# Centring the first token block of a cross-attention and mixture-of-experts kernel before its scale is known, narrowing its last experts, and moving one expert pair to places 28 and 29

## The chip, the cores and the metric

The kernel runs on one core of a Trainium2 chip. Its time is the device time of one execution in microseconds (us). Before the change the median of six runs is 630.84 us (629.49 to 632.16). The engines are named as the profile names them: PE multiplies matrices (PEld is its weight load), DVE works on vectors, ACT computes activations and copies, POOL computes and issues indirect DMAs, SP issues plain DMAs.

## The reference

2048 tokens of width 512 pass through two layers; everything is float32.

```python
x = x + xattn(layernorm(x), expert = min(clip(itok, 0, 24999) // 6250, 3))
#   xattn: y = (silu(h @ C[e].T) * (h @ C[e].T)) @ C[e].T, C = ctx_2048, one of 4 by token
x = x + ffn(layernorm(x))
#   ffn: residual + top-4 of 32 experts of width 256 (silu(g) * u, then w2, weighted)
#        + one shared expert of width 256, on an rmsnorm of its input
```

The layer norm of the first layer has no learned scale: h = (x - mean) * r, with r = (var + 1e-5) ** -0.5, one r for each token.

## The kernel before

The work has three stages, and PE is meant to run through all of them.

**First layer** (from the start to about 170 us). DVE and PE first sort the tokens by expert (L221 to L265); `ident`, a 128x128 identity, is made on the way (L154), and POOL fills `none`, the source of blank rows, with zeros (L163). `turn_over` (L271) is ten, later five, matmuls on sorted data whose results nobody reads. Then 19 blocks of 128 sorted rows are worked on. For a block b: POOL fetches its rows by an indirect DMA (`x_block`, L332); DVE takes mean and variance (`x_moments`, L344 and L345); DVE adds epsilon and POOL raises to the power -0.5 (`x_root`, L351 and L352); DVE makes the scale and bias `rv` (L407, L410) and ACT applies them (`x_norm`, L426), in block 0 with DVE taking one half (L416); PE transposes the block into PSUM and DVE (in block 0 ACT and DVE, a half each) copies it to `xT` (`turn_block`); `up` (L464) multiplies it with the expert's matrix, of which ACT has copied a part to `held` (`hold`, L395); `gate` takes silu on ACT and the product on DVE; `down` (L485) multiplies back, and DVE adds to the rows (L500). Products of `up` have the matrix as the stationary operand and 128 tokens as the moving one, so their result is already transposed for `down`. Block 0 always uses matrix 0, which is read straight from `cT`. PE's order is up(b+1), transposes of b+2, down(b).

**Routing** (about 90 to 265 us, in part under the first layer): second norm, top 4, row numbers, 64 scatters of rows into a table in DRAM, the shared expert (`glu_up`, `glu_down`, `shared`). `ranks` (L791) sorts the 32 experts by how many rows they have: rank 0 has the most. It also counts experts that have more rows than the kernel's limits; if there are any, a slow general path behind the end runs (L1297).

**Experts** (267 us to the end). The 32 ranks are worked on in the order `ORDER`, each at its place, with the first 256 rows as one tile. `up_rank` (L1072) does 32 matmul instructions of `width(r)` columns: 256, and 240 or 228 for the last ranks (`LOW`). `down_rank_by_halves` (L1114) does 14 of 256 columns, by a scheme with seven products of halves; the last rank is done by `down_rank` (L1148). Ranks 0 to 17 may have more than 256 rows; the rest of two ranks (64 rows each) or four ranks (32 each) goes through one common block (`block_up` L1161, `turn_block_act`, `down_block` L1188) at the place of the first of them. ACT and DVE weight the results into `eo`, and `push` (L1042) adds them to the output by an indirect DMA of POOL: two pushes a rank, three if it has part in a common block. The pushes of one rank wait until those of the rank before have landed. A `drain` of POOL stands ahead of place 29 (L1261).

The order of instructions on an engine comes from a scheduler that follows the program and its dependencies; `behind(a, b)` puts a after b by hand.

Of the kernel before, what the change touches and what calls it, by code (L numbers as in the profile page):

```python
# [17 lines left out]
P = 128  # L18
# [25 lines left out]
LOW = ((26, 240), (29, 228))  # L44
# [4 lines left out]
    + [*range(6, 10), 20, 21, 4, 5, 22, 23]  # L49
    + [*range(10, 14), 24, 25]  # L50
    + [*range(14, 18), *range(26, E)]
# [15 lines left out]
def tile_xattn_moe(  # L67
# [95 lines left out]
    nc.gpsimd.memset(none, 0.0)  # L163
# [177 lines left out]

    def x_moments(j):
        st = small.tile([P, nc.vector.BN_STATS_DIM], F32, tag="st", name=f"st_a{j}")
        ins = nc.vector.bn_stats(st, acc[:, j, :])  # L344
        nc.vector.bn_aggr(xmv[:, j, :], st)  # L345
        return ins

    def x_root(j, n=1):
        js = slice(j, j + n)
        ve = small.tile([P, GT], F32, tag="ve", name="ve")  # L350
        nc.vector.tensor_scalar(ve[:, :n], xmv[:, js, 1], LN_EPS, None, ALU.add)  # L351
        ins = nc.gpsimd.tensor_tensor(xr[:, js], ve[:, :n], mhalf[:, 0, :n], ALU.pow)  # L352
        apart(ins, powers, "of blocks before")
        roots.extend([ins] * n)
        in_turn(ins)
# [4 lines left out]
    downs, ups_, turned, turns, halves = [], [], [], [], []  # L360
# [6 lines left out]
    def x_registers(b):  # L367


        if b == 0:  # L370
            off[0] = 0
            regs[0] = 0, 0
            return None
        with queued(downs[-1] if downs else None):

            off[b] = nc.tensor.value_load(be_i[0:1, b : b + 1], min_val=0, max_val=min(b, EX - 1))
        with queued(adds_x[-1] if adds_x else halves[-1] if halves else None):
            dv = nc.vector.value_load(bl_i[0:1, b : b + 1], min_val=0, max_val=NT - 1)
            loaded = nc.cur_bb.bb.instructions[-1]
        with queued(reads[-1] if reads else None):  # L380
            ac = nc.scalar.value_load(bl_i[0:1, b : b + 1], min_val=0, max_val=NT - 1)
        regs[b] = dv, ac
        return loaded

    def hold(b):

        if b == 0:
            held[0] = cT[:, 0]
            return
        with queued(copies[-1] if copies else None):  # L390
            e = nc.scalar.value_load(be_i[0:1, b : b + 1], min_val=0, max_val=min(b, EX - 1))
        held[b] = ctx_pool.tile([P, DC, D], F32, tag="held", name=f"held{b}", bufs=2)
        n = DC // 2
        for h in range(0, DC, n):
            ins = nc.scalar.copy(  # L395
                held[b][:, h : h + n], cT[:, bass.ds(e, 1), h : h + n].rearrange("p o c f -> p (o c) f")
            )
            apart(ins, matrices[b + 1 :], "of experts that come later")
            copies.append(ins)

    def x_norm(b):
# [12 lines left out]
        n = D // 2 if b == 0 else 0  # L414
        if n:
            scaled = nc.vector.tensor_scalar(  # L416
                hn_[b][:, :n],
                acc[:, bass.ds(dv, 1), :n].rearrange("p o d -> p (o d)"),
                rv[:, 0:1],
                rv[:, 1:2],  # L420
                ALU.mult,
                ALU.add,
            )
            apart(scaled, loads[b + 1 :], "of blocks that come later")
            halves.append(scaled)
# [12 lines left out]
    def turn_block(src, tag, name, eng, after_=None):  # L438
        t = xpool.tile([P, DC, P], F32, tag=tag, name=name)
        if eng is None:  # L440
            n, copies = DC // 2, []
            for h, copy in ((0, nc.scalar.copy), (n, nc.vector.tensor_copy)):
                tp = ps_t.tile([P, n, P], F32, tag="tp", name="tp")
                for c in range(n):
                    ins = nc.tensor.transpose(tp[:, c, :], src[:, (h + c) * P : (h + c + 1) * P], ident)
                copies.append(copy(t[:, h : h + n, :], tp))
            turns.append(ins)
            turned.append(copies[1])
            return t, copies[0]
        tp = ps_t.tile([P, DC, P], F32, tag="tp", name="tp")  # L450
        for c in range(DC):
            ins = nc.tensor.transpose(tp[:, c, :], src[:, c * P : (c + 1) * P], ident)
            if after_ is not None:
                behind(ins, after_)
        turns.append(ins)
        turned.append(nc.scalar.copy(t, tp) if eng is nc.scalar else nc.vector.tensor_copy(t, tp))
        return t

    def up(b, fs, after_=None):
        if fs[0] == 0:  # L460
            ups[b] = ps_m.tile([P, DC, P], F32, tag="mm", name="pp")
        pairs = [(f, c) for f in fs for c in range(DC)] if b else [(f, c) for c in fs for f in range(DC)]
        for f, c in pairs:
            ins = nc.tensor.matmul(  # L464
                ups[b][:, f, :],
                held[b][:, c, f * P : (f + 1) * P],
                xT_[b][:, c, :],
                start=(f == 0 and c == 0) if b == 0 else (c == 0),
                stop=(c == DC - 1),
                skip_group_check=(b == 0),  # L470
            )
            if after_ is not None:
                behind(ins, after_)
        ups_.append(ins)

    def gate(b):
        s = xpool.tile([P, DC, P], F32, tag="s", name="s")
        gated.append(nc.scalar.activation(s, ups[b], AF.Silu))
        aT_[b] = xpool.tile([P, DC, P], F32, tag="aT", name="aT")
        made[b] = nc.vector.tensor_tensor(aT_[b], s, ups[b], ALU.mult)  # L480
# [24 lines left out]
    def xattn():  # L505
# [4 lines left out]
        fetched(0, 1, 2)  # L510
        for b in range(2):
            loaded = x_registers(b)
            with tc.issue_after(loaded) if loaded is not None else nullcontext():
                st = x_moments(b)
            behind(st, scaled if b else planned)
            if not b:
                turn_over(5, st)
            x_root(b)
            fetched(3 + b)
            scaled = x_norm(b)  # L520
            if b:
                behind(reads[-1], half_)
            else:
                xT_[0], half_ = turn_block(hn_[0], "xT", "xT", None)
        hold(0)
        up(0, range(DC - 1))
        hold(1)
        xT_[1] = turn_block(hn_[1], "xT", "xT", nc.vector, ups_[0])
        up(0, range(DC - 1, DC), turns[-1])
        gate(0)  # L530
        hold(2)
        for b in range(2, GT):
            st = x_moments(b)
            behind(st, turned[b - 2])
            behind(st, scaled)
            x_root(b)
            fetched(3 + b)
        fetched(GT + 3)
        x_norm(2)
        behind(powers[-1], turned[1])  # L540
        for b in range(XB):
            j = GT * (b // 2 + 1)
            if not b:
                behind(x_moments(GT), made[0])
                x_moments(GT + 1)
            elif j < NT and b % 2 == 0:
# [3 lines left out]
            if b + 3 < XB:  # L550
                x_norm(b + 3)
                if not b:
                    behind(powers[-1], made[0])
            if 0 < b < XB - 2:
                hold(b + 2)
            if b + 1 < XB:
                up(b + 1, range(DC // 2))

# [3 lines left out]
            if b + 1 < XB:  # L562
                up(b + 1, range(DC // 2, DC))
                gate(b + 1)
                if not b:
                    behind(reads[-1], gated[-1])
            n = b - (XB - NT) - 2
            if n >= 0:
                row_ = turn_row(n, ups_[-1])
            if b + 2 < XB:  # L570
                xT_[b + 2] = turn_block(hn_[b + 2], "xT", "xT", nc.vector)
            if not b:
                for i in range(GT + 2, 2 * GT):
                    st = x_moments(i)
                    behind(st, turned[-1])
                x_root(GT, GT)
# [214 lines left out]
    def ranks():  # L791
# [35 lines left out]
        lim = slots.tile([P, E], F32, name="lim")  # L827
        more = slots.tile([P, E], F32, name="more")
        nc.vector.tensor_scalar(lim, rank, float(XA), float(XWA - XWB), ALU.is_lt, ALU.mult)
        nc.vector.tensor_scalar(more, rank, float(XZ), float(XWB), ALU.is_lt, ALU.mult)  # L830
        nc.vector.scalar_tensor_tensor(lim, lim, float(CM), more, ALU.add, ALU.add)
        had = CM
        for r, n in LOW:
            nc.vector.tensor_scalar(more, rank, float(r), float(had - n), ALU.is_ge, ALU.mult)
            nc.vector.tensor_tensor(lim, lim, more, ALU.subtract)
            had = n
        nc.vector.tensor_tensor(lim, n_e, lim, ALU.is_gt)
        over = slots.tile([P, 1], F32, name="over")
        nc.vector.tensor_reduce(over, lim, AX.X, ALU.add)
        over_i = const.tile([P, 1], I32, name="over_i")  # L840
        nc.vector.tensor_copy(over_i, over)
        return er, er_x, er_i, over_i
# [69 lines left out]
    er, er_x, er_i, over_i = ranks()  # L912
    for g in range(G):
        if g:
            aT_s[g], _ = glu_up(h2T[g], shw13, f"s{g}")
        shared(g, aT_s[g])
    while to_put:
# [225 lines left out]
    def down_rank(aT, w2t, wt, to, n, r):  # L1143
        for j in range(MJ):
# [6 lines left out]
            eo = weighted(po, wt[:, j : j + 1], f"{r}_{j}", "eo", m)  # L1151
# [272 lines left out]
```

## Time and profile before

| what | value |
|---|---|
| median of six runs | 630.84 us |
| the profiled execution | 631.29 us |
| its span, first to last instruction | 629.4 us, so 1.9 us lie around it |
| PE, DVE, POOL, ACT busy | 605.5, 401.7, 246.8, 216.5 us |
| first matmul of the sort | 3.91 us |
| first product of block 0 (`up`) | 17.32 us |
| first product of block 1, from which PE is busy | 22.55 us |
| experts' first matmul | 267.40 us |
| last matmul ends | 620.80 us |
| last push issued | 622.01 us |

The page gives each engine's busy time and slices of the span. A timeline lists instructions in order: start, duration, engine, line, operation, what is written from what, and in brackets how long the engine had been idle and what released it. The view of waits adds up such idle times. The chain of waits follows the end back to the start.

### The profile page before, as it was taken

The page shows a single profiled execution, that of the slowest core. Times are in us where ns is not written, and L with a number is a line of the kernel's source. Part 1 is how long each engine was busy: PE and PEld are TensorE (multiplying, and loading weights), DVE is VectorE, ACT ScalarE, POOL GpSimd, SP SyncE. Part 2 cuts the span into 40 slices and gives each one's busy share as a digit, 9 for nine tenths or more (in the row PEclk, how much of TensorE's full clock was granted, in tenths as well). Part 3 has the DMA queues.
Part 4 walks back from the last instruction along what each step waited for, and adds up shares of the span by engine and source line. Part 5 has one row for each costly group of instructions (what it writes and reads, how often), then busy time and mean ns, then how long its engine had stood idle before and what let it go on. Part 6 is the DMA issues. An engine that isn't in the chain of part 4 may idle for free.

```text
span 629.4 us, 10438 instructions
## 1 busy us (share of the span) xinstructions
PE 605.5 (96%) x2962; PEld 434.5 (69%) x2962; DVE 401.7 (64%) x1113; ACT 216.5 (34%) x390; POOL 246.8 (39%) x217
## 2 busy tenths in 40 slices
PE   5899999999996999999999999999999999999994
PEld 2777767777542444477688688858868886888882
DVE  7655556676633822576577677776776778678770
ACT  2435666655321000023222323323332332333331
POOL 4461002366673465414333324234233342524323
PEclk9999999999996999999999999999999999999998
DMA  7489993326272497799989999999999999999434
GB/s 254 148 306 406 414 415 125 120 103 223 103 272 108 171 368 241 210 287 289 299 207 214 272 287 211 215 287 224 248 285 243 212 218 289 237 273 228 68 50 56
DMA packets 104450, 144.55 MB, mean 230 GB/s; under 512 B 21184, under 2 KB 58048, under 8 KB 101824
## 3 DMA queue, kind: packets, MB, share of 16 engines
q1 hardware_dynamic: 86400, 101.54, 53.9%
q0 software_dynamic: 17984, 42.26, 27.5%
q8 instruction: 26, 0.43, 0.3%
q14 instruction: 40, 0.33, 0.2%
HBM read 79.05 MB, written 66.22 MB: 231 GB/s over the span
## 4 chain that ended last, share of the span: by engine, by line
PE 73%; issue 7%; POOL 6%; DVE 5%; DMA 4%; SPq 2%; another core or an unknown queue 1%; ACT 0%; POOLq 0%; DVEq 0%
PE pg L1072 17%; PE pu L1072 16%; PE po L1114 15%; PE pp L464 6%; PE po L485 6%; POOL s_dram L652 4%; PE pp_x L1161 3%; PE po L870 3%; PE pg L855 2%; SPq L940 2%; PE po L1188 2%; PE pu L855 2%; DMA out<-eo,to_all 2%; DMA acc<-in_x,xtok 1%
## 5 line engine op out<-in xcount | busy, mean ns | idle before, releaser
L1042 POOL DMA_INDIRECT out<-eo,to_all x64 | 101.6, 1588 | 218.1 <-DVE eo L1120 95.3
L1072 PE MATMUL pg<-xT,w 128*128 128x256 f32 (+2 forms) x512 | 135.5, 377 | 0.0
L1117 ACT ACTIVATE eo<-po,wt 128x256 f32<-128x256 f32 x124 | 58.4, 473 | 167.1 <-PE po L1114 141.7
L1072 PE MATMUL pu<-xT,w 128*128 128x256 f32 (+2 forms) x512 | 114.0, 376 | 0.0
L1072 PEld LDWEIGHTS pg<-xT,w 128*128 128x128 f32 x512 | 96.6, 190 | 18.5 <-issue 6.2
L1072 PEld LDWEIGHTS pu<-xT,w 128*128 128x128 f32 x512 | 97.3, 190 | 11.5
L652 POOL DMA_INDIRECT s_dram<-h,slot x64 | 62.1, 970 | 36.0 <-issue 16.5
L464 PEld LDWEIGHTS pp<-xT,held 128*128 128x128 f32 x576 | 66.8, 192 | 8.0 <-issue 5.2
L464 PE MATMUL pp<-xT,held 128*128 128x128 f32 x576 | 68.2, 276 | 1.1 <-DVE st_b L611 0.6
L485 PE MATMUL po<-cT,aT 128*128 (+1 forms) x152 | 68.4, 592 | 0.0
L993 DVE STREAM_TRANSPOSE xT<-z 128x1024 f32<-128x1024 f32 x32 | 65.1, 2034 | 0.0
L1120 DVE SCALAR_TENSOR_TENSOR eo<-po,wt,eo 128x256 f32<-128x256 f32 x93 | 45.0, 484 | 24.5 <-PE po L1114 19.8
L1079 DVE TENSOR_TENSOR aT_r<-s,pu 128x256 f32<-128x256 f32 (+2 forms) x64 | 26.5, 414 | 39.0 <-PE pu L1072 30.1
L485 PEld LDWEIGHTS po<-cT,aT 128*128 128x128 f32 x152 | 27.4, 190 | 27.3 <-issue 27.3
L1003 ACT ACTIVATE xT<-xT,nwq 128x256 f32<-128x256 f32 x64 | 29.0, 500 | 46.2 <-DVE xT L993 29.2
L618 POOL TENSOR_TENSOR rs<-rs,mhalf 128x2 f32<-128x2 f32 x16 | 11.3, 704 | 73.0 <-DVE rs L617 73.0
L1095 DVE TENSOR_TENSOR t_r<-w,t_r 128x256 f32<-128x256 f32 x62 | 26.3, 425 | 21.1 <-PE po L1114 20.8
L395 ACT COPY held<-cT 128x1024 f32 x36 | 36.0, 1047 | 10.3 <-DVE valid L312 10.0
L1114 PE MATMUL po<-w,aT_r 128*128 128x256 f32 x124 | 37.8, 386 | 0.1
L1114 PE MATMUL po<-t_r,s_r 128*128 128x256 f32 x124 | 37.6, 385 | 0.0
L1114 PE MATMUL po<-t_r,aT_r 128*128 128x256 f32 x124 | 37.3, 382 | 0.0
L870 PE MATMUL po<-shw,aT_s 128*128 128x512 f32 x64 | 32.8, 651 | 1.5 <-issue 1.1
(203 smaller groups left out, 766.2 us busy)
## 6 DMA issues: line engine op xcount, KB each, us to landing
w<-in_w SPq DMA_DIRECT2D x192, 256.0 KB
s_dram<-none SPq DMA_DIRECT2D x1, 20840.0 KB
z<-s_dram SPq DMA_DIRECT2D x128, 128.0 KB
h_dram<-h SPq DMA_DIRECT2D x4, 1042.0 KB
cT<-in_ctxT SPq DMA_DIRECT2D x4, 1024.0 KB
out<-none SPq DMA_DIRECT2D x1, 1024.0 KB
s_dram<-h,slot POOLq DMA_INDIRECT x64
out<-eo,to_all POOLq DMA_INDIRECT x64
```

What stands on the lines that cost most here:

```text
L395: ins = nc.scalar.copy(held[b][:, h : h + n], cT[:, bass.ds(e, 1), h : h + n].rearrange("p o c f -> p (o c) f"))
L464: ins = nc.tensor.matmul(ups[b][:, f, :], held[b][:, c, f * P : (f + 1) * P], xT_[b][:, c, :], start=(f == 0 and c == 0) if b == 0 else (c ...
L485: ins = nc.tensor.matmul(po, aT_[b][:, f, :], cT[:, bass.ds(off[b], 1), f, :].rearrange("p o f -> p (o f)"), start=(f == 0), stop=(f == DC ...
L652: put = nc.gpsimd.indirect_dma_start(out=table, out_offset=bass.IndirectOffsetOnAxis(ap=index, axis=0), in_=src, in_offset=None,)
L870: ins = nc.tensor.matmul(po, aT[:, f, i * P : (i + 1) * P], w2t[:, f, :], start=(f == 0), stop=(f == IC - 1))
L993: ins = nc.vector.transpose(xT.rearrange("p c (r b) -> p r c b", b=SQ), z.rearrange("p r (a c) -> p r c a", c=DC))
L1003: on_act.append(nc.scalar.mul(xT[:, c, :], xT[:, c, :], nwq[:, c : c + 1]))
L1042: put = nc.gpsimd.indirect_dma_start(out=out, out_offset=bass.IndirectOffsetOnAxis(ap=dst, axis=0), in_=eo, in_offset=None, bounds_check=T ...
L1072: last_up = nc.tensor.matmul(ps, w13t[:, c, f * P : (f + 1) * P], xT[:, c, :n], start=(c == 0), stop=(c == DC - 1))
L1114: return nc.tensor.matmul(ps, L[i], R[i], start=first_, stop=True, skip_group_check=True)
L1117: nc.scalar.mul(eo[i][:, j, :], ps, wt[:, i : i + 1])
L1120: return nc.vector.scalar_tensor_tensor(eo[i][:, j, :], ps, wt[:, i : i + 1], eo[i][:, j, :], ALU.mult, ALU.add)
```

## The change

1. **First block.** Its rows are only centred, half on DVE and half on ACT (`x_centre`); the scale follows later, at the gate (`x_scale`, `gate`). Its `up` is now four products with tokens as the stationary operand and all 512 columns of the matrix moving; the gated result is transposed afterwards by PE (`turn_first`). Both copies of its transposes are ACT's. Block 1 is normed by halves on DVE and ACT and copied by halves on ACT and DVE. Four blocks are fetched ahead, not three; later moments, roots and copies move, and `turn_over` after the first moments is two matmuls, not five.
2. **Blank rows**: `none` is zeroed by ACT, not by POOL.
3. **Narrower last ranks**: `LOW` has widths from rank 20 on. The limits' count, which grows by ten instructions, moves from `ranks` to behind the second group of the shared expert (`limits`).
4. **Order**: ranks 4 and 5, with their common block, go from places 12 and 13 to places 28 and 29; later ones move up.
5. **Last rank**: its results are weighted by halves on ACT and DVE.

```diff
-LOW = ((26, 240), (29, 228))
+LOW = ((20, 252), (22, 248), (24, 244), (26, 240), (28, 234), (29, 228), (30, 224))
 ORDER = (
     [0, 1, 2, 3, 18, 19]
-    + [*range(6, 10), 20, 21, 4, 5, 22, 23]
-    + [*range(10, 14), 24, 25]
-    + [*range(14, 18), *range(26, E)]
+    + [*range(6, 10), *range(20, 24)]
+    + [*range(10, 14), *range(24, 27)]
+    + [*range(14, 18), *range(27, 30)]
+    + [4, 5, 30, 31]
 )
...
-    nc.gpsimd.memset(none, 0.0)
+    nc.scalar.mul(none.rearrange("p j w -> p (j w)"), ones16[:, 0:1].to_broadcast([P, NB * RW]), 0.0)
...
+    def x_centre():
...
+        nc.vector.tensor_scalar(neg[:, 0:1], xmv[:, 0, 0:1], -1.0, None, ALU.mult)
+        hn_[0] = xpool.tile([P, D], F32, tag="hn", name="hn")
+        n = D // 2
+        scaled = nc.vector.tensor_scalar(hn_[0][:, :n], acc[:, 0, :n], xmv[:, 0, 0:1], None, ALU.subtract)
+        halves.append(scaled)
+        reads.append(nc.scalar.activation(hn_[0][:, n:], acc[:, 0, n:], AF.Identity, bias=neg[:, 0:1]))
...
+    def x_scale():
+        ins = nc.vector.tensor_tensor(first_[0][:, 1:2], xr[:, 0:1], valid[:, 0:1], ALU.mult)
...
+                    ps, left, right = ups[b].rearrange("p f t -> p (f t)"), xT_[b][:, c, :], cT[:, 0, c, :]
...
+        gated.append(nc.scalar.activation(s, ups[b], AF.Silu, scale=by))
+        made[b] = nc.vector.scalar_tensor_tensor(s, ups[b], by, s, ALU.mult, ALU.mult)
...
+    def turn_first(after_):
+        aT_[0] = turn_block(first_[1].rearrange("p f t -> p (f t)"), "aT", "aT", nc.vector, nc.vector, after_=after_, whole=True)
...
-        fetched(0, 1, 2)
...
+        fetched(0, 1, 2, 3)
+        st = x_moments(0)
+        behind(st, planned)
+        turn_over(2, st)
+        scaled = x_centre()
+        xT_[0] = turn_block(hn_[0], "xT", "xT", nc.scalar, nc.scalar)
+        half_ = turned[-1]
+        x_root(0)
+        loaded = x_registers(1)
+        with tc.issue_after(loaded):
+            st = x_moments(1)
+        behind(st, scaled)
+        x_root(1)
+        fetched(4)
+        scaled = x_norm(1)
+        behind(reads[-1], half_)
+        behind(x_scale(), scaled)
+        halves.append(scaled)
+        up(0, range(DC - 1))
+        hold(1)
+        xT_[1] = turn_block(hn_[1], "xT", "xT", nc.scalar, nc.vector, after_=ups_[0])
...
+        up(0, range(DC - 1, DC), turns[-1])
+        hold(2)
+        behind(copies[2], first_half)
...
                 up(b + 1, range(DC // 2, DC))
+                if not b:
+                    turn_first(ups_[-1])
                 gate(b + 1)
...
+        if g == 1:
+            over_i = limits(adds_s[-1])
...
-            eo = weighted(po, wt[:, j : j + 1], f"{r}_{j}", "eo", m)
+            eo = last.tile([P, D], F32, tag="eo", name=f"eo_{r}_{j}", bufs=EO)
+            nc.scalar.mul(eo[:m, :HD], po[:m, :HD], wt[:m, j : j + 1])
+            nc.vector.tensor_scalar(eo[:m, HD:], po[:m, HD:], wt[:m, j : j + 1], None, ALU.mult)
             push(eo[:m, :], to[:m, j : j + 1], f"rank{r}")
```

## The prediction

> **What bounds the kernel now.** I read the page first, then PE's waits, then timelines of the three places that the change touches.
>
> ```profile
> PE 605.5 (96%) x2962; PEld 434.5 (69%) x2962; DVE 401.7 (64%) x1113; ACT 216.5 (34%) x390; POOL 246.8 (39%) x217
> ...
> PEclk9999999999996999999999999999999999999998
> ```
>
> PE is busy for 605.5 of 629.4 us. PE's waits cut to the experts' stage (266 to 622 us) have a single entry of 0.3 us: there every column that PE doesn't process is time saved, and work of other engines costs nothing while PE has no wait. The other 24 us lie at three places: before PE has steady work (22.55 us), at 187 to 203 us (the dip to 6 in the clock row), and after its last matmul (8.6 us). The change works on the first and the third, and on PE's column count.
>
> **The head: POOL's fill.** A stretch of the timeline from 1.4 us:
>
> ```profile
> 1.26 0.28 DVE L148 TENSOR_SCALAR tri<-iota_q,row_b 128x128 f16<-128x128 f32 x1
> ...
> 1.53 1.99 DVE L154 TENSOR_SCALAR ident<-iota_q,row_b 128x128 f32<-128x128 f32 x1
> 1.59 1.85 POOL L163 MEMSET none<- 128x2084 f32 x1
> ...
> 2.44 1.19 DVE L226 TENSOR_SCALAR ge<-tok_sb 128x16 f16<-128x16 int32 x3
> ```
>
> `ident` takes 1.99 us where its twin `tri` takes 0.28, and it ends just after POOL's memset. The first `ge` starts at 2.44 and is held until 3.54 (1.10 us, the two others 0.10 and 0.15). With the fill on ACT, the three `ge` end near 2.8 instead of 3.63, and all that follows (matmul at 3.91, sort, first fetch on POOL at 10.07) comes some 0.85 us sooner. Bounds: nothing, if something else holds DVE, and 1.0, if the `ge` were instant. ACT's fill is about 2.1 us (a copy of 1024 columns takes 1.05) and lies in ACT's idle time from 2.2 to 12.2 us; without that cover it would delay `held`. Does the fetch land sooner too? In windows of 1 us the three matrices keep the DMA at 393 GB/s until 11 us and leave 80 GB/s in the next; the rows' packets would start about there. I pass on the whole 0.85; nothing is the other end. The Trainium skill ("DMA: Bandwidth & Descriptors", Queues, rings and completion order) says that a DMA engine takes turns between rings packet by packet, which speaks against this step: sharing the last 0.3 us of the matrices' traffic would take some 0.15 us from it, an estimate.
>
> **The first block.** From the timeline of 13.5 to 23 us:
>
> ```profile
> 13.71 0.69 DVE L344 BATCH_NORM_STATS2 st_a<-acc 128x6 f32<-128x512 f32 x1 [1.41 <-DMA acc<-in_x,xtok]
> 14.44 0.18 DVE L345 BATCH_NORM_AGGREGATE xmv<-st_a 128x2 f32<-128x6 f32 x1
> ...
> 14.90 0.58 POOL L352 TENSOR_TENSOR xr<-ve,mhalf 128x1 f32<-128x1 f32 x1 [1.12 <-DVE ve L351]
> ...
> 15.90 0.41 DVE L416 TENSOR_SCALAR hn<-acc,rv 128x256 f32<-128x256 f32 x1
> ...
> 16.96 0.69 DVE L344 BATCH_NORM_STATS2 st_a<-acc 128x6 f32<-128x512 f32 x1 [0.65 <-DMA acc<-in_x,xtok]
> ...
> 17.32 2.90 PE L464 MATMUL pp<-xT,cT 128*128 128x128 f32 x24
> ...
> 17.57 0.41 DVE L446 COPY xT<-tp 128x256 f32<-128x256 f32 x1
> ...
> 19.62 0.81 ACT L426 ACTIVATE hn<-acc,rv 128x512 f32 x1 [1.07 <-DVE rv L410]
> 20.49 0.66 PE L452 MATMUL tp<-ident,hn 128*128 128x128 f32 x4 [0.28 <-ACT hn L426]
> ...
> 22.55 0.71 PE L464 MATMUL pp<-xT,held 128*128 128x128 f32 x4 [0.50 <-DVE xT L456]
> ```
>
> Block 0: from the end of the moments (14.62) to DVE's half (16.31) pass 1.69 us, through `ve`, POOL's power and two `rv`. Centred, it is a negation (next start some 0.1 later) and the same 0.41: 0.55. So `up(0)` starts 1.1 earlier by this and 0.85 by the head: about 15.35. But its first three products last only 6 x 0.43 = 2.6 us (a 512-column instruction starts every 0.43 in L485's rows); PE is then through at 17.95 and block 1 is late next.
>
> Block 1 therefore sets the gain. Today its moments start at 16.96, on landing, and its `up` at 22.55: 5.59 us. In it DVE copies a half of block 0 (17.57), which pushes `ve` back; block 0's undisturbed rows take 2.19 from moments to `hn` (13.71 to 15.90), block 1's 2.66. ACT does the whole block (0.81), and DVE's copy waits behind another block's moments (0.50 of PE). After: 2.19, ACT's half 0.60, two transposes with their starts 0.3, the last product of `up(0)` 0.86, under which both copies (0.37 and 0.41) hide: 3.95. That is 1.64 less, so with the head `up(1)` starts at 22.55 - 0.85 - 1.64 = 20.06, after a PE gap of about 0.8 us. If the scheduler sets a `held` copy of 1.05 ahead of `hn`, the gap covers most of it; without the gap it costs 1.05.
>
> Against it stand the four transposes of `turn_first`: 4 x 0.11 = 0.44 on PE. Its DVE copies (0.41 each) lie under the four transposes of block 2. The four wide products replace 32 short instructions (3.57 us) by 8 x 0.43 = 3.44, inside what is counted. Sum of the front: -0.85 - 1.64 + 0.44 = **-2.05**; its ends are -0.8 (fetch unmoved, a little lost to order) and -2.6. POOL's root of block 3 now waits for `turn_first`'s copies, so fetches 6 and 7 are issued some 1.7 later (26.07 to 27.8) and block 4 is normed by about 35 us; PE transposes it near 39. Without those 4 us it would cost what is missing. The blank rows' 20.8 MB go out about 1.2 later, and the first scatter at 120.80 has room.
>
> Fewer `turn_over` matmuls are off the path. They matter for the clock: ten took 4.45 us at 9.83, the next five 1.33 from 14.46, half the time each. The Trainium skill ("TensorE: Matmul & The Clock Gate", Part 1 and Part 4) has the full clock follow one busy window of about 3.4 us that runs free, and transposes not count as busy. This speaks against fewer matmuls and a gap: one window late would cost up to 1.7 us, an estimate; the ten matmuls alone are longer than a window. No term here uses it.
>
> **Narrower ranks.** From PE's timeline:
>
> ```profile
> 556.94 3.62 PE L1072 MATMUL pu<-xT,w 128*128 128x256 f32 x16
> ...
> 576.30 3.40 PE L1072 MATMUL pu<-xT,w 128*128 128x240 f32 x16
> ...
> 604.75 3.24 PE L1072 MATMUL pu<-xT,w 128*128 128x228 f32 x16
> ```
>
> From `pu` to the next `pu` a plain rank takes 9.93 us at 256 columns (388.89 to 398.82), 9.57 at 240 (566.73 to 576.30), 9.37 at 228 (604.75 to 614.12): 22 and 20 ns a column. The change takes 4, 8 and 12 columns from two ranks each, 6 from rank 28 and 4 from 30 and 31. 54 x 22 ns = 1.2; for the last eight I take 0.05, as 228 columns cost 192 ns an instruction and the weight load beside it 190. Sum **-1.25**, from -1.1 to -1.67 (62 x 32 x 0.84 ns). Six more memsets of 95 ns lie in DVE's 36% of idle time. By the reference's routing the ranks 20 to 31 have 247, 245, 243, 240, 240, 239, 229, 223, 221, 210, 201 and 195 rows, within the new widths, so the general path doesn't run. `limits`, 21 short DVE instructions of some 0.2, goes into DVE's idle 6.25 us ahead of 232.27; SP reads the result at 231.3 and its next rows are fetched at 242, so it costs nothing; without that room it would hold the z fetches.
>
> **The pair and the end.** A common block costs PE the same anywhere. Its cost is in pushes:
>
> ```profile
> 605.04 1.55 POOL L1042 DMA_INDIRECT out<-eo,to_all  x1 [6.88 <-issue]
> ...
> 612.63 1.55 POOL L1042 DMA_INDIRECT out<-eo,to_all  x1 [4.17 <-DVE eo L1120]
> ...
> 619.11 0.69 ACT L1037 ACTIVATE eo<-po,wt 128x512 f32<-128x512 f32 x1 [4.19 <-PE po L1148]
> ...
> 620.14 1.56 POOL L1042 DMA_INDIRECT out<-eo,to_all  x1 [4.09 <-ACT eo L1037]
> ```
>
> The last ranks' first pushes are 7.59 and 7.51 us apart: 1.86 between the two, then landing (619.36 in the chain of waits) and 0.78 to the next. PE's results come 8.98 apart, then 7.81. With three pushes the spacing is 10.4 to 11.0 where loads run (545.65, 556.67, 567.08, 577.87). At place 29 the loads are over (SP's last is at 580.61), and a third of 64 rows adds about 1 us: 8.5, below 9. I take 8.5, the quiet rows being nearer; at 10.8 rank 31 is 1.5 late. The drain ran to 604.17, some 7.6 after the last push before it; after place 28 the common block's 6.7 us of PE cover that. The last weighting falls from 0.69 to 0.48, but the push at 620.14 waits also for the landing at 619.36: **-0.1**, between -0.3 and +1.5.
>
> **Sum.** -2.05 - 1.25 - 0.1 = -3.4. The profiled execution, 631.29 us with 1.9 around the span, lies 0.45 above the median of 630.84; it would become 627.9 (span 626.0), the median **627.4**. About 0.2% (1.26 us) is what a measurement can tell from no change.
>
> **How it could go.**
>
> - *As summed*, 0.52: 627.4, own range 626.2 to 629.1 by the ends above.
> - *The front gives nothing*, 0.16: the fetch lands no sooner (+0.85) and the first block runs at the half rate of the ten matmuls (+1.5 of its 3.4 us): 629.8. For it: the same DMA engines carry the fourth matrix; against: DMA falls to 80 GB/s at 11 us.
> - *Pushes hold the end*, 0.11: 10.8 between ranks 5 and 30, +1.5: 628.9.
> - *The stall at 187 us goes*, 0.06: PE does next to nothing from 189 to 196 with no wait that explains it. Its loss is some 9 us; a different instruction stream may miss it: 618.
> - *Slower*, 0.15: the clock falls between the second `turn_over` and `up(1)`. In windows around the stall it is 0.86 at 190 to 193, 0.50 to 200, 0.60 to 203, so about 10.2 us at half, from 192.2 on, after a stretch from 188.8 almost without matmuls. In the front that costs up to 5.1: 632.5, and more than 3.4 from about 6.8 us at half clock. It decides once the gap of 0.8 us grows to some 3 (block 1's rows landing 2 us late). Against it: no such gap today.
>
> Faster: 0.52 + 0.06 + 0.09 of the push case + 0.04 of the second = 0.71; same: 0.12 + 0.02 = 0.14; slower 0.15. The range leaves out the stall's case (0.06) and most of the slower one (0.12): 625.8 to 631.4.
>
> **What will show it.** Right: `ident` near 0.3 us, first fetch near 9.2, `up(0)` near 15.4, `up(1)` near 20.1, 9.57 or less from place to place for ranks 20 to 31 where they have no block, last push some 3.4 earlier. Wrong: `ident` still 2 us; moments of block 1 still at 16.96; a clock below 1 before 30 us; more than 9 us between the first pushes of ranks 5 and 30; new PE waits after 30 us.

## The result and the profile after

The changed kernel takes 632.0 us (median of 20 runs, 630.86 to 634.01), the kernel before 630.29 us (46 runs, 628.77 to 632.16). The ratio is 1.003, with a 95% interval of 1.0022 to 1.0037: slower by 0.3%. The forecast was 627.4 us, its range 625.8 to 631.4. The profiled execution took 632.07 us, with a span of 630.3; that of the kernel before, at 631.29, lies 1.0 above its median, so the two profiles differ by 0.8 us where the medians differ by 1.7.

One thing is needed to read the numbers below: the kernel before took 630 to 632 us beside the runs above and beside seven of the experiments, and 622 us beside the other eight, one chip showed both, and every ratio is to the kernel before in the same set of runs ("beside 630" and "beside 622" say which).

The page, to be held against the two rows of before:

```profile
PE 605.4 (96%) x2939; PEld 433.6 (69%) x2939; DVE 405.3 (64%) x1133; ACT 219.8 (35%) x394; POOL 245.5 (39%) x216
...
PEclk9998999999996999999999999999999999999998
```

The 23 instructions less are the shorter `turn_over` (3) and the wide products (24), with the four transposes of `turn_first` added, and the sum of PE's busy time hardly moved. The clock row has a new 8 in its fourth slice, at 47 to 63 us. The front itself, from the timeline (start, duration, and in brackets how long the engine had been idle and what released it):

```profile
1.54 0.28 DVE L155 TENSOR_SCALAR ident<-iota_q,row_b 128x128 f32<-128x128 f32 x1
2.48 0.33 DVE L227 TENSOR_SCALAR ge<-tok_sb 128x16 f16<-128x16 int32 x3 [0.66 <-DMA tok_sb<-in_tok]
...
13.15 0.69 DVE L347 BATCH_NORM_STATS2 st_a<-acc 128x6 f32<-128x512 f32 x1 [1.68 <-DMA acc<-in_x,xtok]
...
15.52 2.79 PE L484 MATMUL pp<-cT,xT 128*128 128x512 f32 x6
...
19.80 3.73 PE L484 MATMUL pp<-xT,held 128*128 128x128 f32 x32
...
24.27 0.44 PE L464 MATMUL tp<-ident,s 128*128 128x128 f32 x2 [0.52 <-DVE aT L468]
```

Up to block 1's `up` at 19.80 (22.55 before) all of it came within 0.3 us of the forecast. Then PE's milestones turn round:

| start of | before | after | difference |
|---|---|---|---|
| `up` of block 0 | 17.32 | 15.52 | -1.80 |
| `up` of block 1 | 22.55 | 19.80 | -2.75 |
| `down` of block 0 | 26.66 | 24.98 | -1.68 |
| `up` of block 3 | 37.53 | 35.85 | -1.68 |
| `up` of block 4 | 45.09 | 47.12 | +2.03 |
| `up` of block 5 | 52.61 | 56.26 | +3.65 |
| experts' first matmul | 267.40 | 270.78 | +3.38 |
| first `pu` of the last rank | 614.12 | 616.12 | +2.00 |
| last push | 622.01 | 624.20 | +2.19 |
| end of the span | 629.4 | 630.3 | +0.9 |

So the change gains 1.68 us in the front, loses 5.33 between 39 and 56 us, gets 0.27 back up to the experts and 1.38 from the first rank to the last, loses 0.19 up to the last push and gains 1.29 behind it. The loss in the timeline, engine by engine:

```profile
39.43 0.60 PE L464 MATMUL tp<-ident,hn 128*128 128x128 f32 x4
39.86 3.60 PE L507 MATMUL po<-cT,aT 128*128 x8
43.61 0.96 POOL L333 DMA_INDIRECT acc<-in_x,xtok  x1 [0.30 <-issue]
45.52 0.60 ACT L492 ACTIVATE s<-pp 128x512 f32<-128x512 f32 x1 [5.58 <-remote]
46.28 0.69 DVE L468 COPY xT<-tp 128x512 f32<-128x512 f32 x1 [7.33 <-remote]
47.12 1.64 PE L484 MATMUL pp<-xT,held 128*128 128x128 f32 x11 [3.66 <-ACT held L391]
```

PE's transposes of block 4 stand at 39.43 to 40.03, and the copy of their result starts at 46.28. DVE had been idle for 7.33 us; what released it is given as "remote", that is, the trace found no instruction. The trace's records of PE's signals stand at 45.50 and 46.26, just ahead of the two starts, so the two engines were released by PE, late. ACT's silu of block 3 had waited 5.58 us for products that PE's records end at 39.59. PE then waits 3.66 us for the copy (the label names ACT's `held`; the copy at 46.28 to 46.97 is what ends last). The line of POOL is the last of eight fetches in a row, 34.72 to 44.57. After the wait the clock falls. By windows (the window and its length, the busy time of PE, PEld, DVE, ACT and POOL with their instructions, the granted clock, the DMA share, GB/s):

```profile
48.20:51.70 3.50, 3.50 (x19) 3.50 (x18) 3.29 (x11) 0.00 (x0) 0.07 (x1) 0.51 0.67 269
```

That is 3.5 us at half clock: block 4's 32 products and the transposes to the next start take 5.44 us, not 3.81. That is 3.66 + 1.63 = 5.29 of the 5.33.

The kernel before had the same late results in the same place, and hardly a wait. Its timelines of POOL, ACT, DVE and PE:

```profile
41.32 0.96 POOL L332 DMA_INDIRECT acc<-in_x,xtok  x1 [0.30 <-issue]
...
44.25 0.60 ACT L478 ACTIVATE s<-pp 128x512 f32<-128x512 f32 x1 [7.27 <-remote]
...
42.90 0.69 DVE L344 BATCH_NORM_STATS2 st_a<-acc 128x6 f32<-128x512 f32 x1 [0.34 <-DMA acc<-in_x,xtok]
...
44.25 0.69 DVE L456 COPY xT<-tp 128x512 f32<-128x512 f32 x1
...
45.09 1.13 PE L464 MATMUL pp<-xT,held 128*128 128x128 f32 x8
```

Its row of fetches ends at 42.28, its transposes at 41.71, and PE's signals for silu and copy are recorded at 44.17 and 44.23. But here the copy could hardly have come sooner: DVE has the moments of the fetched rows ahead of it, waits for their landing (42.90) and is busy until 44.13. Beside 622 us (`before_again`) silu starts at 40.73 with no such delay, and the copy still only at 43.79. The changed kernel has these moments behind the copy, so there PE's late signal is all that the copy waits for. PE's `up` at 45.09 follows the start of the `down` ahead of it by 3.55 us, where its neighbours take 3.43 or 3.44: it was already 0.12 us late.

### The profile page after: what moved, and what is told of

It is laid out like the page before. It is cut to its first block, busy times and chain, and to the rows that moved or that the text cites. A ratio compares the mean times of both kernels' runs of the same rounds, so it can differ in the third digit from the quotient of the medians.

```text
span 630.3 us, 10421 instructions
## 1 busy us (share of the span) xinstructions
PE 605.4 (96%) x2939; PEld 433.6 (69%) x2939; DVE 405.3 (64%) x1133; ACT 219.8 (35%) x394; POOL 245.5 (39%) x216
## 4 chain that ended last, share of the span: by engine, by line
PE 68%; issue 10%; POOL 7%; DMA 6%; DVE 4%; another core or an unknown queue 2%; ACT 1%; POOLq 0%; ACTq 0%; DVEq 0%
PE pg L1118 15%; PE pu L1118 14%; PE po L1160 13%; PE pp L484 6%; PE po L507 4%; DMA out<-eo,to_all 4%; PE po L914 4%; POOL s_dram L690 3%; PE pu L899 3%; PE pg L899 3%; PE pp_x L1209 3%; PE po L1236 1%; DMA acc<-in_x,xtok 1%; POOL out L1088 1%
## 5 line engine op out<-in xcount | busy, mean ns | idle before, releaser
L1118 PE MATMUL pg<-xT,w 128*128 128x256 f32 (+7 forms) x512 | 134.9, 375 | 0.0
L1118 PE MATMUL pu<-xT,w 128*128 128x256 f32 (+7 forms) x512 | 113.1, 374 | 0.0
L484 PEld LDWEIGHTS pp<-xT,held 128*128 128x128 f32 x576 | 68.5, 196 | 11.4 <-issue 5.1
L484 PE MATMUL pp<-xT,held 128*128 128x128 f32 x576 | 69.7, 280 | 4.2 <-ACT held L391 3.7
L1125 DVE TENSOR_TENSOR aT_r<-s,pu 128x256 f32<-128x256 f32 (+7 forms) x64 | 26.4, 412 | 37.0 <-PE pu L1118 32.6
L1141 DVE TENSOR_TENSOR t_r<-w,t_r 128x256 f32<-128x256 f32 x62 | 26.5, 427 | 21.2 <-PE po L1160 20.8
```

The costliest lines, as they stand in the source:

```text
L484: ins = nc.tensor.matmul(ps, left, right, start=(c == 0), stop=(c == DC - 1))
L1118: last_up = nc.tensor.matmul(ps, w13t[:, c, f * P : (f + 1) * P], xT[:, c, :n], start=(c == 0), stop=(c == DC - 1))
```

## The experiments

Theory A: the row of eight indirect DMAs holds back PE's results (or PE) until about its end. The change ends the row 2.3 us later, in part since POOL's root of block 3 waits for the copies of `turn_first` (without the two lines that order this, `root3_early_2` below ends it 1.1 sooner), and wants the result 1.7 us sooner. Theory B: the mere traffic of the DMA engines does it, which were full from 36 to 47 us. Theory C: the order of the work around block 4.

**The first four runs** came beside a kernel before of 622.03 us. `split`:

```diff
-                fetched(*range(2 * GT, NT))
+                fetched(*range(2 * GT, 3 * GT))
                 second_inputs(st)
-                blanks(loads[-1])
+            if b == 3:
+                for j in range(3 * GT, NT):
+                    x_block(j)
+                    behind(loads[-1], adds_x[-1], mybir.DependencyClass.Sync)
+                blanks(loads[-1])
```

> The changed kernel with the last eight fetches of rows cut in two: blocks 8 to 11 as before, blocks 12 to 15 (and the blank rows that wait for them) only after block 2's rows are added. In the changed kernel PE stands from 43.46 to 47.12, then runs at half clock for 3.4 us; the results that DVE and ACT wait for came 5.9 us after the matmuls that the trace shows. Theory A (the eight indirect DMAs of POOL in a row, 34.72 to 44.56, hold back PE's results or PE itself until about their end): with four of them the release comes near 40, PE has no wait before block 4's up, its up stands near 43.5 instead of 47.12, no half clock near 48, time 632.0 - 5.3 = 626.7. Theory B (the amount of DMA traffic, the shared expert's weights above all): the wait stays to within 1.5 us, 630.5 or more. Theory C (the order of DVE's and ACT's work around block 4): nothing changes, 632.

`inputs_late`:

```diff
-                second_inputs(st)
                 blanks(loads[-1])
+                second_inputs(loads[-1])
```

> The changed kernel with the loads of the shared expert and the blank output rows (2.6 MB, on SP at 31.9 to 35.6 us) issued behind the long write of blank rows instead of ahead of it; the eight fetches in a row stay. Theory A (the eight fetches in a row): PE's wait before block 4's up stays, 3 to 3.7 us, 632. Theory B (DMA traffic: 16 engines full at 36 to 47 us in the changed kernel, and not without these loads): the wait goes, up of block 4 near 43.5, no half clock near 48, 626.7. Theory C (order of work): nothing changes, 632.

`root3_early`:

```diff
-                    behind(aggrs[3], turned[-1])
...
-                    behind(made[1], ves[3])
```

> The changed kernel without the two lines that put block 3's variance and its epsilon behind the copies of the turned first block, so that POOL's root of block 3, the fetches 6 and 7 and the eight fetches after them come about 1.2 us sooner. Theories A and B alike: the release of PE's results moves with the burst, from 45.5 and 46.3 to about 44.3 and 45.1, PE waits 1.2 us less (2.4 us) and may keep its clock: 629 to 631. If the lateness of the burst is not what costs (theory C), 632.

`back_only` is the kernel before with the parts 3 to 5 of the change alone:

```diff
-LOW = ((26, 240), (29, 228))
+LOW = ((20, 252), (22, 248), (24, 244), (26, 240), (28, 234), (29, 228), (30, 224))
...
-    + [*range(14, 18), *range(26, E)]
+    + [*range(14, 18), *range(27, 30)]
+    + [4, 5, 30, 31]
```

> The kernel before with only the narrower ranks, the new order, the moved count of limits and the last rank's halves; first layer as before. My prediction's terms give 630.3 - 1.25 - 0.1 = 628.9. The changed kernel's trace, compared place by place, gives 1.38 from the first to the last rank and 1.1 at the end that may be chance: 628.9 or 627.8. If these parts cost, and not the first layer, it is 631 or more.

Measured: split 617.51 us, ratio 0.9921 (0.9906 to 0.9935); root3_early 617.83, 0.9931 (0.9915 to 0.9948); back_only 619.97, 0.9959 (0.9943 to 0.9975); inputs_late 648.67, 1.0416 (1.0398 to 1.0434). None of the four shows a wait before block 4's `up`, and none the dip of PE at 187 us that before has. So split and root3_early tell nothing apart here. inputs_late missed for a reason of its own, which its waits of PE name:

```profile
PE tp L464 <- ACT h2T L686: 26.7, 1, 26.7
```

The norm weights lay behind 20.8 MB on SP's queue, and ACT needed them for `h2T`. back_only gives 2.1 us: more than the 1.35 of my terms.

**The kernels themselves in such a set.** `after_again` and `before_again` are without edits; `front_only` is the kernel before with the parts 1 and 2 of the change:

```diff
-    nc.gpsimd.memset(none, 0.0)
+    nc.scalar.mul(none.rearrange("p j w -> p (j w)"), ones16[:, 0:1].to_broadcast([P, NB * RW]), 0.0)
...
-        fetched(0, 1, 2)
+        fetched(0, 1, 2, 3)
```

`inputs_mid` has the second inputs in another place:

```diff
-                second_inputs(st)
-                blanks(loads[-1])
+            if b == 3:
+                last_ = second_inputs(adds_x[-1])
+                behind(blanks(loads[-1]), last_)
```

> The changed kernel itself, once more, with a profile. In the last four runs the kernel before took 622.0, not 630.3, and no variant showed PE's dip at 187 us or a wait at 43 us. Theory D (what cost at 43 to 52 us is a standstill of PE's results that some chips or executions show and others don't, not the change's own work): where the kernel before takes about 622, the changed kernel has no wait before block 4's up and takes 622.0 - 2.0 (back) - 1.7 (front) = 618.3; where before takes about 630, PE's wait of 3.7 and the half clock are there again, 632. Theory A (the burst is late by itself): wait there on any chip, 623.5 where before takes 622.

> The kernel before itself, for a profile on the same chip as its neighbours. Theory D: if it takes about 622, no dip of PE at 187 to 203 us and full clock there; if it takes about 630, the dip as in the first profile.

> The kernel before with only the changes of the first layer (centred block 0, blank rows filled by ACT); order, widths and last rank as before. By the trace of the changed kernel the front gains 1.68 us up to block 3, and then loses 5.3 at 39 to 52 us. Where the kernel before takes about 622: 620.3 by theory D, 625.6 by theory A. Where it takes about 630: 634 by both.

> The changed kernel with the loads of the shared expert, the norm weights and the blank output rows (2.6 MB) only after block 2's rows are added, and ahead of the long write of blank rows; the eight fetches in a row stay. (In inputs_late they came behind that write, and PE waited 26.7 us for the norm weights; here they come ahead of it.) Where the kernel before takes about 630: by theory A (eight fetches in a row) PE's wait of 3.7 us before block 4's up stays, 632; by theory B (DMA traffic) it goes, 626.7. Where it takes about 622 there is no such wait in any case by theory D: 618.3, as the changed kernel.

Measured, beside a kernel before of 622.08: **after_again 617.92 us, ratio 0.9938 (0.9922 to 0.9954)**, before_again 622.11, front_only 621.81, 0.9993 (0.9981 to 1.0004), inputs_mid 617.8, 0.9929 (0.9914 to 0.9944). The same changed kernel that is slower by 0.3% beside 630 is faster by 0.6% beside 622. In its profile the copy that started at 46.28 starts right behind the transposes (39.21 to 39.81), though POOL issues the same row, here until 44.23, and the DMA engines are as full (0.98 to 1.08 from 36 to 46 us):

```profile
39.84 0.69 DVE L468 COPY xT<-tp 128x512 f32<-128x512 f32 x1 [1.05 <-PE tp L464]
43.08 3.18 PE L484 MATMUL pp<-xT,held 128*128 128x128 f32 x27
```

PE has no gap. Theory C falls, since the order is the same, and theories A and B fall as causes that act in every run. Theory D holds: the standstill is there in some runs and not in others. What is left to tell apart is what brings it where it is there. Held instruction by instruction against after_again, PE in the recorded execution falls back at two places only, by 5.5 us at 43 to 52 and by 9.2 at 186 to 205. front_only missed: 621.8, not 620.3. Its profiled execution has PE's last matmul 1.40 us before that of before_again and a span 2.6 shorter, but the other runs spread from 620.3 to 623.2, and why is open.

**Beside 630 us.** split again:

> The kernel of split once more, for where the kernel before takes about 630 us (in the runs so far beside it took 622, and neither it nor the changed kernel showed a wait at 43 us or a dip at 187). Where before takes about 630: theory A (the eight indirect DMAs in a row bring the standstill of PE's results) says no wait before block 4's up, 626.7, ratio 0.994; theory B (traffic of the DMA engines as such) says a wait of more than 2 us and a ratio of 1.000 to 1.003. Where before takes 622: 617.5 as the first time, and nothing is told apart.

Measured: 627.48 us beside 631.07, **ratio 0.9932 (0.9909 to 0.9956)**. POOL, DVE and PE:

```profile
39.45 0.96 POOL L333 DMA_INDIRECT acc<-in_x,xtok  x1 [0.30 <-issue]
...
41.60 0.69 DVE L468 COPY xT<-tp 128x512 f32<-128x512 f32 x1 [1.50 <-PE tp L464]
...
44.11 3.73 PE L484 MATMUL pp<-xT,held 128*128 128x128 f32 x32
```

The row ends at 40.41, the copy starts 1.19 later, PE does not wait, and the clock stays whole there. The DMA engines were full until 46 us (1.03 in the window of 42 to 44). So B falls, and the row is left, as theory A says. The dip at 187 to 201 us is there.

Then the other half, the row without the traffic:

> The kernel of inputs_mid again (the changed kernel with the 2.6 MB of second inputs only after block 2's rows are added; the eight fetches in a row stay), for where the kernel before takes about 630 us. There, split had no wait at 43 us although the DMA engines were full until 46 us, so traffic alone does not bring the standstill. If the row of eight indirect DMAs alone brings it: the wait of 2 to 3.7 us before block 4's up stays, ratio 1.000 to 1.003. If it takes both, the row and full DMA engines: no wait, ratio about 0.993. Where before takes 622: 617.8, and nothing is told apart.

Measured: 632.43 us beside 631.4, ratio 1.0025 (1.0009 to 1.0041). By windows the DMA engines are 0.56 to 0.70 busy from 36 to 46 us, and PE's wait before block 4's `up` is 3.75 us:

```profile
42.00:44.00 2.00, 1.43 (x4) 0.36 (x2) 0.00 (x0) 0.00 (x0) 1.39 (x3) 1.00 0.67 213
```

The row brings it without full DMA engines. Next, whether the wait lasts as long as the row. `row6` is split with 6 and 2 fetches for 4 and 4:

```diff
-                fetched(*range(2 * GT, 3 * GT))
+                fetched(*range(2 * GT, 3 * GT + 2))
...
-                for j in range(3 * GT, NT):
+                for j in range(3 * GT + 2, NT):
```

> The changed kernel with the row of eight fetches cut to six, the last two (and the blank rows) after block 2's rows are added. If PE's results are held until the row ends (44.56 in the changed kernel, first result at 45.50): the row ends near 42.0, results come at 42.5 to 43.9, PE waits at most 1.5 us before block 4's up (3.66 in the changed kernel) and its clock stays whole: ratio about 0.993 to 0.996 where the kernel before takes 630. If a hold of fixed length starts after some number of DMAs under seven: wait still over 3 us, 1.000 to 1.003. Where before takes 622: 617.5 to 618.3.

> The kernel of root3_early again (fetches 6 and 7 and the row of eight some 1.3 us sooner), for where the kernel before takes 630. If the results are held until the row ends: the row ends near 43.2, PE waits 1.3 us less (about 2.3), and with the shorter wait the half clock of 3.4 us may not come: 629 to 631, ratio 0.996 to 1.001. If the lateness is not the cause: 632, 1.003. Where before takes 622: 617.8.

Measured beside 631.82: row6 627.92 us, ratio 0.9934 (0.9913 to 0.9955); root3_early_2 628.91, 0.9956 (0.9929 to 0.9982). PE's timeline of root3_early_2:

```profile
45.98 2.91 PE L484 MATMUL pp<-xT,held 128*128 128x128 f32 x15 [2.17 <-DVE xT L468]
```

Six of the profiles beside 630, in order of the row's end (last start of a fetch and its duration):

| kernel | row ends | copy of block 4 starts | behind the row | PE waits |
|---|---|---|---|---|
| split_2 | 40.41 | 41.60 | 1.19 | 0 |
| before | 42.28 | 44.25 | 1.97 | 0 |
| row6 | 43.11 | 44.41 | 1.30 | 0.84 |
| root3_early_2 | 43.47 | 45.14 | 1.67 | 2.17 |
| after | 44.57 | 46.28 | 1.71 | 3.66 |
| inputs_mid_2 | 44.66 | 46.34 | 1.68 | 3.75 |

The copy follows the end of the row by 1.2 to 2.0 us, wherever that end lies, and in each of the six PE's signal is recorded 0.02 to 0.03 us ahead of it. (In before DVE's own order would have held it until 44.13 too.) The later the row ends, the longer the wait: theory A, by size. A hold of fixed length, row6's rival, falls. Two expectations were off in size: row6's row ended at 43.11, not near 42.0, as its whole front ran 1 us later, and root3_early_2 came out just below its 629 to 631. Its five runs spread from 628.0 to 631.0; the profiled one is among the longest, and in it the clock fell again behind the wait of 2.17, while row6's wait of 0.84 left it whole.

What the rest of the change gives here:

> The kernel of back_only again (order, widths, limits, last rank's halves; first layer as before), for where the kernel before takes 630. As beside 622, where its ratio was 0.996: 2.0 us less than before, ratio 0.995 to 0.998, no wait at 43 us. Then the first layer's changes alone make the changed kernel slower there, by some 3.7 us.

Measured: 628.73 us, ratio 0.9955 (0.9941 to 0.997). So the parts 3 to 5 give 2.8 us, and the first layer's parts cost 1.003 - 0.9955, some 4.7 us. With the row cut they seem to gain: split_2 against back_only_2 is 0.9932 against 0.9955, 1.5 us, but the two intervals overlap.

**The dip at 187 us** is the same thing if theory A is right: POOL issues thirteen scatters in a row there, 176.51 to 192.73 in split_2. `paced` is split with half as many released in the first group of the shared expert, `paced2` makes up for it in the later groups:

```diff
-                    if c % 2:
+                    if c % 2 if name != "s0" else c == DC - 1:
                         step(ins)
```

```diff
-                    if c % 2:
+                    if (c == DC - 1 if name == "s0" else c % 2 or (f == 0 and c == 0 and ps is pg)):
                         step(ins)
```

> The kernel of split, and the scatters of the second half released at half the pace in the first group of the shared expert (after every fourth matmul instruction pair, not every second), so that POOL no longer issues thirteen in a row at 176 to 193 us. Where before takes about 630: if a row of more than some eight indirect DMAs brings the standstill at 187 to 201 us, PE loses at most 3 of the 10 us there: 617 to 620, ratio 0.978 to 0.984, clock 1.0 throughout. If something else at this place brings it, 627.5 as split. Where before takes 622: 617.5, within 0.5 of split, as there is slack behind the scatters.

> The kernel of paced with the four rows of the base put back into the paced sequence of the later groups, so that no row of ten indirect DMAs stands at 253 to 263 us. In paced PE lost 1.4 us at 188 and not 10.2, but 2.2 at 254 (beside that row) and 2 to 4 more on weights that came late. If rows of indirect DMAs are what costs: no loss at 254, 619 to 622 where the kernel before takes 630, ratio 0.982 to 0.986. If the loss at 254 has another cause: as paced, 623.5. Where before takes 622: 617 to 618.

Measured: paced 623.48 us beside 631.4, ratio 0.9876 (0.982 to 0.9932); **paced2 619.68 beside 631.82, ratio 0.9804 (0.9778 to 0.9831)**. The clock row of paced2, and 188 to 192 us by windows in split_2 and in paced2:

```profile
PEclk9999999999999999999999999999999999999999
```

```profile
188.00:192.00 4.00, 1.88 (x4) 0.48 (x3) 0.69 (x1) 0.00 (x0) 3.09 (x4) 0.92 0.52 202
```

```profile
188.00:192.00 4.00, 3.34 (x10) 1.58 (x11) 2.84 (x18) 1.79 (x4) 1.00 (x2) 1.00 0.26 101
```

PE is busy for 3.34 of the 4 us, not 1.88, and nearly 9 us that split_2 then loses are gone. So the row of thirteen brings the dip. paced2's longest row there still has eight scatters, 175.39 to 185.27, and PE's wait behind it is 0.7 us. paced missed its 617 to 620: its profile has PE some 4.7 us behind that of paced2. Eight puts of the base were left in a row at 252.70 to 263.28, but PE's wait beside them is only 0.81 us (0.32 at the same place in paced2, where they are spread); most of the rest arises later, up to the matmuls at 341 and 501 us, in part in waits for weights, so the row at 253 us is not shown to be what paced2 gains by. paced2 came as expected (619 to 622 us, its ratio just below 0.982), and beats both kernels beside 630 us: 12.1 us under before. Beside 622 it was not run.

## Why the prediction was wrong

**The step that failed.** "POOL's root of block 3 now waits for `turn_first`'s copies, so fetches 6 and 7 are issued some 1.7 later (26.07 to 27.8) and block 4 is normed by about 35 us; PE transposes it near 39. Without those 4 us it would cost what is missing." The overlap was wrong. Each number in it came nearly true: fetch 7 at 27.59, block 4 normed at 35.41 to 36.22, its transposes at 39.43. The step stopped there. Behind fetches 6 and 7 stand the moments of blocks 6 and 7, the root of four blocks (31.21 to 33.50) and the row of eight fetches (32.43 to 34.72), and it is this row that the result of the transposes waits for. I counted 4 us of cover at the transposes; at the copy there were none. In the profile of before PE's `up` of block 4 already came 0.12 us late behind it (the 0.15 from the copy's end at 44.94 to 45.09 are no slack: they are there too where PE waited, 46.97 to 47.12). In place of the cover the runs showed a wait of 3.66 us and 1.63 us lost to the half clock. The sign was in the profile of before: ACT's silu at 44.25, 7.27 us idle and released by nothing that the trace names, 3.0 us behind its products (37.53 to 41.26). The copy alone, 2.5 us behind its transposes, would not have told, as DVE's own order put it there. The Trainium skill ("Perfetto Trace Analysis", Summary: the profiler window per engine type) says that the end of a matmul in a profile is an estimate and that the way of its signal is not shown. Here 5.9 us lie between a recorded end (39.59) and the first use (45.52), and 0.3 for the same products beside 622; whether the end or the signal was late, the trace doesn't tell. Cover is to be read at the consumer's start.

**Head.** First fetch -0.83 (9.24 for 10.07), as worked out at 0.85. The rows landed 0.56 earlier, not 0.85. I passed on the whole; the share of 0.15 that I worked out from the skill's rule on rings, and left out of the sum, had the right sign and half the size; whether the sharing brought it, no run here shows.

**First block.** `up` of block 0 at 15.52 (forecast 15.35), from block 1's moments to its `up` 4.06 (3.95), `up` of block 1 at 19.80 (20.06). Right in this pair, and partly by luck: block 1's rows landed 1.22 us sooner, not 0.85, and the 5.59 us of before from which I took 1.64 are its profile's own. In the three other profiles with the old first layer it is 4.97, as DVE's copy there doesn't wait behind another block's moments; with the new one it is 4.05 to 4.16 in twelve of thirteen. Over these seventeen profiles `up` of block 3 starts at 37.17 in the mean with the old first layer and at 36.05 with the new one, so the front gives 1.1 us rather than the pair's 1.68.

**`turn_first`.** Forecast 0.44; the gain fell from 2.75 to 1.68, by 1.07. The line at 24.27 shows what was missing: the second pair of transposes waits 0.52 for the copy of the first, as both halves have one PSUM tile (`whole=True`). I had put the copies "under the four transposes of block 2", and they are not. Front in all -1.68 in this pair for -2.05, inside its ends, as is the mean of -1.1.

**Narrower ranks.** -1.25 forecast, -1.38 measured from the first to the last rank (343.27 to 341.88), and -1.37 in the pair beside 622. Two ranks of PE's timeline, at 234 and 228 columns:

```profile
561.51 3.32 PE L1118 MATMUL pu<-xT,w 128*128 128x234 f32 x16
570.95 3.24 PE L1118 MATMUL pu<-xT,w 128*128 128x228 f32 x16
```

From place to place it is 9.55 at 240 columns (551.96 to 561.51), 9.44 at 234, 9.31 at 224 (606.81 to 616.12): 13 to 18 ns a column at the narrow end, where I had counted 0.05 us for eight columns.

**Pair and end.** First pushes of ranks 5 and 30 are 9.30 apart, forecast 8.5, and above the 9 that I had named as wrong. The pushes did not hold the end: the first of rank 30 was released by DVE's `eo`, and PE's own spacing there is 9.72 (597.09 to 606.81). From the last rank's `pu` to the last push it is 8.08 for 7.89: +0.19 for my -0.1, inside the bounds. The step that failed here: I let the two halves of the last weighting run side by side (0.48 for 0.69). They run one behind the other, ACT from 621.06 to 621.53 and DVE, which the trace has waiting for ACT, from 621.57 to 622.05: 0.99 in all, so part 5 costs some 0.2 to 0.3 us. The span ends 4.65 us behind the last push's end, not 5.77. In the three profiles with the old order this is 5.5 to 6.1, in all that have the new one 4.65 to 5.25. Some 0.8 us that no term had; which edit brings it wasn't tried.

**The rivals.** The slower case had the right time, 632.5, and the wrong place: I let the clock fall before block 1's `up`. It fell at 48 us, for some 3.4 us, after a wait that none of my cases had, and cost 1.63. The Trainium skill's window of about 3.4 us ("TensorE: Matmul & The Clock Gate", Part 1), from which the prediction took an estimate of up to 1.7, fits that. "New PE waits after 30 us" was what I had named as showing the forecast wrong, and that is what came. The case in which the stall at 187 us goes is real, but the change doesn't do it: paced and paced2 do.

**What was right.** Where the row holds nothing, the total comes near the forecast: -4.4 us between the spans of before_again and after_again (620.3 to 615.9), of it -1.46 up to the first `pu`, -1.37 in the ranks and -1.57 from the last `pu` on; the ratio 0.9938 has the forecast's 627.4 / 630.84 = 0.9945 in its interval. Of the three terms only that of the ranks was right; that the sum meets is luck, as the front gave less than forecast and the end 1.5 us that no term had. The medians beside 622 don't even show the front: front_only is 0.3 us under before, within noise.

## What to carry to other kernels

When a change delays what an engine issues, follow that queue to its end: the price lay in the eight fetches behind the two that I had followed, and it was due only in runs where such a row holds results back. Measure cover where a result is used, not where it is recorded as made; an idle consumer whose releaser the profile can't name, long after its producer's end, marks a result that is held up. And break long rows of indirect DMAs where another engine waits for PE: four at a time cost nothing here, eight cost between nothing and 3.75 us of waiting with a slow clock behind it, thirteen some 9.

## What the runs showed of the hardware

- Beside 630 us, a row of POOL's indirect DMAs (one each 1.26 us) can hold back what PE has made until after the row's end: the copy of block 4 starts 1.2 to 2.0 us behind it (1.0 to 1.2 in paced and paced2, with four in a row); beside 622 us the same row holds nothing (39.84 against 46.28 for the same copy). What makes the two kinds of runs isn't known. The traces differ in one more thing: those beside 630 have 563 to 587 records of PE's signals, those beside 622 649 to 652. The records are missing in paced2 (570) as well, where PE hardly waits.
- It isn't every row: beside eight scatters at 220.25 to 230.07 in the changed kernel PE, DVE and ACT keep their distance of 14.98 us from after_again to within 0.02. Why is open, and so is whether PE itself stands or only its signals.
- A wait of 3.66 us of PE, and one of 2.17, brought half the clock for 3.4 us; one of 0.84 did not.
